# Convolution matrices built in parts, taps on other queues, and three smaller moves in the first two stages of a ConvNeXt block followed by a selective scan

## The chip, the core and the metric

The kernel runs on one core of a Trainium2 chip, in float32. The metric is device time in microseconds of one execution, and a time stands for the median of several runs. A profile is one execution recorded by the hardware profiler; its times start at the span's beginning.

## The reference, cut to what matters

Two layers, one after the other. The input x is (32, 96, 56, 56).

```python
# layer 0
h = depthwise_conv7x7(x, conv_w) + conv_b
h = layernorm over the 96 channels (ln_g, ln_b)
h = gelu(h @ w1 + b1)              # 96 -> 384
h = (h @ w2 + b2) * layer_scale    # 384 -> 96
x = h + x
# layer 1
x = silu(depthwise_conv5x5(x, conv_w) + conv_b)
dts, Bs, Cs = split(x_proj_w @ x)
delta = softplus(dt_w @ dts + dt_b)
P = exp(cumsum(max(delta * -exp(A_logs), log(1e-9))))
hs = P * cumsum(delta * Bs * x / max(P, 1e-9))
y = sum over n of hs * Cs, + x * Ds
```

The change touches layer 0, the convolution of layer 1, and the matrices of taps that both convolutions use. The scan is as it was.

## The kernel before, in words

**Units of work.** The batch is cut into two halves (g = 0, 1) of 16 images, 96 channels into 24 groups of four. A block n is one group of four channels of one half, all rows and columns. Blocks 0 to 47 are the first convolution (24 for each half), 48 to 95 the second. `convolve` multiplies the rows of a block, loaded on 31 partitions of each quarter, by banded matrices that hold the taps of a channel at every row offset; 7x7 takes 64 matmuls a block (8 column offsets x 4 quarters x 2), 5x5 takes 48. A float32 matmul appears in a profile as two passes, each with a weight load. One row of the 31 is a row of ones, which brings the bias in, and therefore the x tiles are filled with 1.0 once before the first load.

**The matrices.** `taps` loads the taps into `kt`, four times, once for each quarter of the partitions, by eight DMAs. `shifts` makes `tap` (the taps in reversed order) and `sel` (shifted identities), and returns `build`, which multiplies the two on TensorE into PSUM and copies the result into `ws[k]` (tile `w7s` or `w5s`). `bands` copies the two matrices of a block from there into the layout that `convolve` reads, on ScalarE, one or two blocks ahead.

**PSUM.** All of this work takes its PSUM from `slot`: two slots of four banks each, so all eight banks. Whoever takes a slot waits until the last reader of the one two before it is done.

**Order.** `pin` keeps every engine's instructions in program order, so the order of the code is each engine's order. Loads are issued on the queue of SP, stores on that of GpSimd, and the taps on that of ScalarE.

**First half of the time, as stages.**
- Blocks 0 to 23: a loop of `block1` (load ahead, convolve, copy to `ht` on ScalarE, store to conv1_d), `square` on ScalarE and `gather_sums` on VectorE, four additions of 128x896 into `acc`. Small setup steps of the MLP and the scan are hung behind some blocks (`later`). All matrices are built before the loop.
- The norm: blocks 24 and 25 with `norm(0)` between. It sums over the partitions by TensorE (`pm`), takes the variance and square root, and two reciprocals into `rstd_t`.
- Steps u = 0 to 56 of the MLP, `half_u` = 28 for each half. A step does, in order: `spread_norm(u+1)` (one matmul that spreads rstd into bank 3 of the slot `po`), `second(u-1)` (36 matmuls, 384 to 96), `normed(u+1)` (three multiplications on VectorE), `residual(u-1)` (bias and x, three operations on VectorE; after every second step four stores of `o` to block_d), then a block if there is one, then three times `expand` (12 matmuls and a Gelu on ScalarE). The tile `o` has one buffer; `h`, `x` have two.
- In u = 0 to 21 the block is one of 26 to 47 (first convolution, second half). In u = 22 to 27 there is no block: the second stage's taps are loaded (u = 22), `norm(1)` is done (u = 23), `shifts` (u = 24) and the matrices (u = 25 to 27). u = 28 and 29 have no block either. In u = 30 to 49 the block is one of 48 to 67 (second convolution, first half), whose Silu reads PSUM directly, with `table` loading the function's table ahead of it and the Gelu's again after it. u = 50 to 56 have no block.
- Then blocks 68 to 95 without MLP, and the scan, which takes the second half of the time.

Of the kernel before, what the change touches and what calls it, by code (L numbers as in the profile page):

```python
# [44 lines left out]
def convnext_then_scan_kernel(  # L45
# [58 lines left out]
    def taps(tmp, cw, cb, k):  # L104
        s = k + 1
        kt = tmp.tile([128, C, k], F32, name=f"kt{k}")
        pin(nc.vector.memset(kt, 0.0))
        for q in range(Q):
            lo = q * PR
            pin(nc.scalar.dma_start(  # L110
                kt[lo : lo + k], cw.rearrange("c (i u) -> i c u", i=k)
            ))
            pin(nc.scalar.dma_start(
                kt[lo + k : lo + s, :, k // 2 : k // 2 + 1],
                cb.rearrange("(o c u) -> o c u", o=1, u=1),
            ))
        return kt

    def shifts(pool, tmp, kt, k, z, zs, down):
        s = k + 1  # L120
        tap = tmp.tile([128, C, s], F32, name=f"tap{k}")
        pin(nc.vector.memset(tap[:, :, 0:1], 0.0))
        for v in range(1, s):
            pin(nc.vector.tensor_copy(tap[:, :, v : v + 1], kt[:, :, k - v : k - v + 1]))
# [18 lines left out]
        for q in range(Q):  # L143
            rows = slice(q * PR, (q + 1) * PR)
            pin(nc.vector.tensor_copy(
                sel[rows, :, :, PR - 1],
                ident[rows, q * PR + k : q * PR + s].rearrange("p (a o) -> p a o", a=1)
                .to_broadcast([PR, 2, PR]),
            ))
        wt = pool.tile([128, 2 * KB, PR * s + 1], F32, name=f"w{k}s")  # L150
# [3 lines left out]
        def build(lo, hi):  # L154
            for a in range(lo, hi):
                ps = slot(f"pw{k}_{a}")
                for i in range(Q):
                    cp, h = divmod(i, 2)
                    for b in range(Q):
                        base = tap[b * PR : b * PR + s, cp]  # L160
                        pin(nc.tensor.matmul(
                            ps[i * PR : (i + 1) * PR, b, : 2 * KB * s],
                            lhsT=sel[b * PR : b * PR + s, h, a * Q + b],
                            rhs=bass.AP(
                                base.tensor, base.offset, [base.ap[0], [2 * s, 2 * KB], [1, s]]
                            ),
                            start=True, stop=True, tile_position=(b * PR, i * PR),
                        ))
                dst = wt[:, :, a * Q * s : (a + 1) * Q * s].rearrange("p n (b v) -> p b n v", v=s)
                src = ps[:, :, : 2 * KB * s].rearrange("p b (n v) -> p b n v", v=s)  # L170
                if a % 2:
                    pin(nc.vector.tensor_copy(dst, src))
                else:
                    pin(nc.scalar.copy(dst, src))
# [216 lines left out]
    def conv(n):  # L391
# [10 lines left out]
        if k == K1:  # L402
            pin(nc.scalar.copy(ht, ps[:, :, :TOK]))  # L403
            for j in range(2):
                pin(nc.gpsimd.dma_start(  # L405
                    at(conv1_d[g], (kb * 4 + 2 * j) * CS,
                       [[2 * TOK, 64], [CS, 2], [1, 2 * TOK]]),
                    ht[j * 64 : (j + 1) * 64].rearrange("p (c h) w -> p c (h w)", c=2),
                ))
        else:  # L410
            pin(nc.scalar.activation(ht, ps[:, :, :TOK], AF.Silu))  # L411
            for j in range(2):
                for r in range(2):
                    rows = slice(j * 64 + r * PR, j * 64 + (r + 1) * PR)
                    pin(nc.gpsimd.dma_start(  # L415
                        at(conv2_d[g], (kb * 4 + 2 * j) * CS + r * 2 * TOK,
                           [[4 * TOK, PR], [CS, 2], [1, 2 * TOK]]),
                        ht[rows].rearrange("p (c h) w -> p c (h w)", c=2),
                    ))
        return ht  # L420

# [17 lines left out]
    def norm(g):  # L439
        acc = accs.pop(g)  # L440
# [11 lines left out]
        pin(nc.scalar.activation(m2, m2, AF.Sqrt, bias=eps_t, scale=1.0))  # L452
        for h in range(2):
            pin(nc.vector.reciprocal(rstd_t[:, g, h], m2[:, h]))
# [102 lines left out]
    def residual(u, po):  # L557
        n, s = divmod(u, 2)
        g, h, o = spot(n)
        for e in range(3):  # L560
            pin(nc.vector.scalar_tensor_tensor(  # L561
                ots[n][:, e].rearrange("p (t s) -> p t s", s=2)[:, :, s],
                in0=po[:, e, :TOK], scalar=b2p_t[:, e : e + 1],
                in1=xrs[n][:, e].rearrange("p (t s) -> p t s", s=2)[:, :, s],
                op0=ALU.add, op1=ALU.add,
            ))
# [17 lines left out]
    with tc.tile_pool(name="early", bufs=1) as early, tc.tile_pool(  # L584
        name="w1t", bufs=1, side="right"
    ) as tmp:
        kt = taps(tmp, c1w, c1b, K1)
        fresh += [early.tile([128, 2, COLS], F32, name=f"xe_{i}") for i in range(4)]
        for i, t in enumerate(xts + fresh):
            (nc.gpsimd if i % 2 else nc.vector).memset(t, 1.0)  # L590
        shifts(w1pool, tmp, kt, K1, Z1, (3, 0), False)(0, PR // Q)
        later = {
            2: lambda: setup_loads_mlp(tmp),
            4: setup_sums,
            6: lambda: setup_mlp_0(tmp),
# [8 lines left out]
        for n in range(KB):  # L604
            squares, sums = block1(n, half_n)
            squares()
            sums()
            if n in later:
                later[n]()
# [5 lines left out]
    for n in range(KB, KB + lead):  # L615
        squares, sums = block1(n, half_n)
        if n == KB:
            norm(0)
        squares()
        sums()  # L620
    load_x(0)
    load_h(1)
    load_x(1)

    half_u = B2 * OCT * 2
    n1, n2 = KB + lead, half_n
    start = slot("po_first")
    spread_norm(0, start[:, 3])
    normed(0, start[:, 3])
    for u in range(2 * half_u + 1):  # L630
        if u or u + 1 < 2 * half_u:
# [3 lines left out]
            if u:  # L635
                second(u - 1, po)
            if u + 1 < 2 * half_u:
                normed(u + 1, po[:, 3])
            if u:
                residual(u - 1, po)  # L640
        squares = sums = None
        if u < half_u:
# [3 lines left out]
            elif u == half_u - 6:  # L646
                wstack.close()
                w2pool = wstack.enter_context(tc.tile_pool(name="w2p", bufs=1, side="right"))
                temps = ExitStack()
                tmp = temps.enter_context(tc.tile_pool(name="w2t", bufs=1, side="right"))  # L650
                kt = taps(tmp, c2w, c2b, K2)
            elif u == half_u - 5:
                norm(1)
            elif u == half_u - 4:
                build2 = shifts(w2pool, tmp, kt, K2, Z2, (0, 3), True)
            else:
                at_ = {3: 0, 2: 3, 1: 6}.get(half_u - u)
                if at_ is not None:
                    build2(at_, min(at_ + 3, PR // Q))
                    if u == half_u - 1:  # L660
                        temps.close()
        elif u == half_u + 1:
            ahead(half_n, half_n + KB)
        elif u >= half_u + 2 and n2 < half_n + KB - TAIL:
            ahead(n2, half_n + KB)
            conv(n2)
            table(AF.Gelu)
            n2 += 1
        if u < 2 * half_u:
# [4 lines left out]
            if half_u + 2 <= u + 1 and n2 < half_n + KB - TAIL:  # L674
                table(AF.Silu)
# [303 lines left out]
```

## Time and profile before

| | us |
|---|---|
| median of 3 runs | 3306.44 (3301.59 to 3317.9) |
| the profiled execution | 3315.05 |
| its span | 3313.3 |
| block 0 begins on PE | 36.93 |
| first expansion of u = 0 | 235.66 |
| second layer's first block (48) begins | 852.74 |
| last residual ends | 1350.4 |
| scan's first matmul | 1540.7 |

| engine | busy us | share |
|---|---|---|
| PE, matmuls | 2882.4 | 87% |
| PE, weight loads | 1041.9 | 31% |
| DVE | 2129.6 | 64% |
| ACT | 1948.7 | 59% |
| POOL | 1765.8 | 53% |

How to read it. PE is TensorE, DVE VectorE, ACT ScalarE, POOL GpSimd, SP SyncE. A line of the timeline has the start, the duration, engine, line of the kernel, operation, output <- inputs, shapes and a count; in brackets stands the idle time of the engine before it and what ended it. A line of the windows has the stretch, and for each engine the busy time and count in the order PE, PEld, DVE, ACT, POOL, then the granted clock, the share of the DMA engines and GB/s. The names drop the numbers of buffers: `kt` stands for kt7 and kt5, `xc` and `xe` are tiles of x for a block, `we` the bands, `pc`, `po`, `ph`, `pm`, `pw` are slots named after their use.

### The profile page before, as it was taken

To read this page: it belongs to the slowest core of one execution; us is meant where nothing else is said; L and a number is where in the kernel's file an instruction comes from. 1 tells how busy PE (TensorE), PEld (TensorE's weight loads), DVE (VectorE), ACT (ScalarE), POOL (GpSimd) and SP (SyncE) were. 2 spreads that over 40 slices of the span, in tenths; PEclk is the share of its full clock that TensorE was granted. 3 is DMA by queue.
4 is the path that set the end of the run, shared out by engine and by line. 5 is a ranking of instruction groups with operands and counts; after the bars stand their busy time and mean duration, and the time that the engine had idled before them with its cause. 6 is when DMAs were issued, how large, how long until landed. Compare 5 with 4: busy or idle time off the path is not lost.

```text
span 3313.3 us, 65909 instructions
## 1 busy us (share of the span) xinstructions
PE 2882.4 (87%) x28172; PEld 1041.9 (31%) x28172; DVE 2129.6 (64%) x1227; ACT 1948.7 (59%) x1915; POOL 1765.8 (53%) x904
## 2 busy tenths in 40 slices
PE   7989999988999999988887888788888888887885
PEld 5544444433344443442222222222222222222221
DVE  4763333332111112100999999999999999999998
ACT  5864444433555553444766666666667666766673
POOL 2311111100111110232988988898889888987896
PEclk9999999999999999997777778777777877877776
DMA  9997666533876664697655465636564666455642
GB/s 177 267 235 210 183 185 182 168 96 109 224 199 188 190 189 126 192 280 197 179 155 148 145 184 138 165 130 182 143 173 125 183 158 157 135 174 151 161 137 87
DMA packets 363619, 563.64 MB, mean 170 GB/s; under 512 B 221728, under 2 KB 292400, under 8 KB 363328
## 3 DMA queue, kind: packets, MB, share of 16 engines
q1 hardware_dynamic: 332352, 432.29, 48.8%
q0 software_dynamic: 25424, 127.03, 12.7%
q8 instruction: 222, 3.64, 0.5%
q10 hardware_dynamic: 5552, 0.12, 0.1%
q14 instruction: 69, 0.57, 0.1%
HBM read 355.58 MB, written 203.69 MB: 169 GB/s over the span
## 4 chain that ended last, share of the span: by engine, by line
PE 45%; DVE 23%; ACT 10%; POOL 7%; DMA 5%; SPq 5%; issue 4%; ACTq 0%; POOLq 0%; DVEq 0%
PE pc L324 13%; PE po L551 11%; DVE run_t L844 9%; DVE u L852 9%; PE ph L532 8%; DVE run_t L848 5%; POOL da L859 3%; PE px L755 3%; POOL u L839 3%; PE py L871 2%; PE pz L772 2%; ACT da L830 2%; PE py L866 2%; PE pd L825 2%; SPq L383 2%
## 5 line engine op out<-in xcount | busy, mean ns | idle before, releaser
L839 POOL TENSOR_TENSOR u<-u,bc 128x1568 f32<-128x1568 f32 x192 | 674.8, 3515 | 209.2 <-DMA u<-dx_d 196.6
L844 DVE TENSOR_TENSOR_SCAN run_t<-da,run_t 128x1568 f32<-128x1568 f32 x192 | 664.5, 3461 | 68.1 <-ACT da L834 49.3
L859 POOL TENSOR_TENSOR da<-u,bc 128x1568 f32<-128x1568 f32 x192 | 674.5, 3513 | 18.8 <-DVE u L852 18.4
L524 DVE TENSOR_TENSOR h<-h,po 128x448 f32<-128x448 f32 x165 | 92.6, 617 | 588.6 <-PE po L551 554.2
L532 PE MATMUL ph<-h,w1c_t 32*128 32x448 f32 x4032 | 410.9, 551 | 29.1 <-ACT g L538 17.0
L830 ACT ACTIVATE da<-pd,lift_t,a_t 128x784 f32<-128x784 f32 x384 | 377.9, 1003 | 74.5 <-PE pd L825 64.2
L825 PE MATMUL pd<-dl,rep_t 32*128 32x392 f32 x1536 | 387.3, 641 | 32.9 <-ACT bc L807 13.7
L538 ACT ACTIVATE g<-ph,b1p_t 128x1792 f32<-128x1792 f32 x168 | 291.7, 1750 | 179.2 <-PE ph L532 160.3
L551 PE MATMUL po<-g,w_t 128*32 128x448 f32 x4032 | 390.5, 540 | 0.0
L866 PE MATMUL py<-xs,dsm_t 32*32 32x392 f32 x1536 | 251.4, 734 | 143.1 <-ACT bc L807 108.6
L324 PE MATMUL pc<-xc,we 32*64 32x432 f32 (+2 forms) x6912 | 357.6, 554 | 11.7 <-DVE h L524 7.6
L848 DVE SCALAR_TENSOR_TENSOR run_t<-run_t,u 128x1568 f32<-128x1568 f32 x192 | 345.6, 1800 | 22.2 <-POOL u L839 2.1
L571 POOL DMA_DIRECT2D block_d<-o x112 | 59.8, 557 | 547.8 <-DVE o L561 532.1
L803 PE MATMUL pk<-xd,pick_t 32*128 32x392 f32 x1024 | 270.5, 642 | 92.0 <-ACT y L877 76.5
L852 DVE TENSOR_TENSOR_SCAN u<-da,u,run_t 128x1568 f32<-128x1568 f32 x96 | 334.1, 3480 | 3.4
L852 DVE TENSOR_TENSOR_SCAN u<-da,run_t 128x1568 f32<-128x1568 f32 x96 | 328.3, 3420 | 3.3
L834 ACT ACTIVATE da<-da,lift_t 128x1568 f32<-128x1568 f32 x192 | 307.8, 1603 | 5.6
L871 PE MATMUL py<-da,sel_t 128*32 128x392 f32 x1536 | 248.4, 733 | 53.4 <-POOL da L859 53.4
L405 POOL DMA_DIRECT2D conv_d<-ht x96 | 57.1, 600 | 417.4 <-ACT ht L403 407.4
L532 PEld LDWEIGHTS ph<-h,w1c_t 32*128 32x128 f32 x4032 | 202.1, 188 | 238.0 <-issue 168.8
L415 POOL DMA_DIRECT2D conv_d<-ht x192 | 101.3, 535 | 316.5 <-ACT ht L411 292.2
L877 ACT COPY y<-py 128x392 f32<-128x392 f32 x192 | 92.0, 479 | 289.5 <-PE py L871 228.0
(118 smaller groups left out, 2993.4 us busy)
## 6 DMA issues: line engine op xcount, KB each, us to landing
u<-dx_d SPq DMA_DIRECT2D x192, 784.0 KB, 5.1
conv_d<-ht POOLq DMA_DIRECT2D x96, 448.0 KB, 6.0
conv_d<-ht POOLq DMA_DIRECT2D x192, 224.0 KB, 5.1
h<-conv_d SPq DMA_DIRECT2D x336, 112.0 KB, 2.8
x<-in_x_dram SPq DMA_DIRECT2D x112, 336.0 KB, 8.8
block_d<-o POOLq DMA_DIRECT2D x112, 336.0 KB, 7.1
xs<-conv_d SPq DMA_DIRECT2D x384, 98.0 KB, 4.0
dx_d<-dx SPq DMA_DIRECT2D x256, 147.0 KB, 3.3
```

What stands on the lines that cost most here:

```text
L324: pin(nc.tensor.matmul(pv[:, :, lo:hi], lhsT=wt[rows, j, k - d], rhs=xv[rows, j, :, lo + e : hi + e, s], start=(t == 0), stop=(t == k), ti ...
L532: pin(nc.tensor.matmul(ph[:, q, :TOK], lhsT=w1c_t[quarter(q), e, f * 128 : (f + 1) * 128], rhs=ht[quarter(q), e, s], start=(e == 0), stop= ...
L551: pin(nc.tensor.matmul(po[quarter(q), e, :TOK], lhsT=w2_t[:, f, e * PR : (e + 1) * PR], rhs=gts[u, f][:, q], start=(f == 0), stop=(f == 2) ...
L825: pin(nc.tensor.matmul(ps[:, j, :BK], lhsT=rep_t[quad(q)].rearrange("p c n -> p (c n)"), rhs=dls[b, h][quad(q), g], start=True, stop=True, ...
L830: pin(nc.scalar.activation(pair(da, a), ps[:, :, :BK], AF.Relu, bias=lift_t[:, 0:1], scale=a_t[:, g : g + 1],))
L839: pin(nc.gpsimd.tensor_mul(us[i], us[i], bcs[b, h, 0]))
L844: pin(nc.vector.tensor_tensor_scan(run_t[:, 1 : T + 1], da, zero, run_t[:, T : T + 1] if h else 1.0 / EPS, ALU.mult, ALU.add,))
L848: pin(nc.vector.scalar_tensor_tensor(run_t[:, :T], in0=run_t[:, 1 : T + 1], scalar=1.0, in1=ut, op0=ALU.min, op1=ALU.mult,))
L852: pin(nc.vector.tensor_tensor_scan(ut, da, run_t[:, :T], last["h"] if h else 0.0, ALU.mult, ALU.add))
L859: pin(nc.gpsimd.tensor_mul(das[i], us.pop(i), bcs[b, h, 1]))
L866: pin(nc.tensor.matmul(py[quad(j)], lhsT=dsm_t[quad(j), g], rhs=tokens(b, h, quad(j), g), start=True, stop=False, tile_position=(j * PR, j ...
L871: pin(nc.tensor.matmul(py[quad(j)], lhsT=sel_t, rhs=hc[:, j * BK : (j + 1) * BK], start=False, stop=True, tile_position=(0, j * PR),))
```

## The change

Five things change.
1. The matrices are built in parts. `build(n0, cnt, a0, per)` now makes `cnt` groups from `n0`, and `4 * per` offsets from `a0`, in one slot. A matmul has cnt x s columns (64 or 128 in the first stage, 144 in the second, instead of 384 and 288), and there are 512 instead of 128 in the first stage and 256 instead of 128 in the second. A slot is emptied in two halves, one by ScalarE and one by VectorE. In the first stage only groups 0 to 7 are built before block 0; five more parts follow blocks 0, 1, 4, 6 and 10. In the second stage six parts stand in u = 23 to 28.
2. The taps go by ScalarE's and SP's queues in turn in the first stage, by SP's alone in the second. All tiles of ones are filled by GpSimd, and `tap` is made after the shifted identities.
3. In steps with no block (u = 22 to 29 and 50 to 56, where `mixed` is false) ScalarE adds the bias, reading PSUM and writing `o`, and GpSimd then adds x.
4. In u = 30 to 49 ScalarE copies the block raw out of PSUM, and Silu runs in place behind the step's three Gelus, with its table loads and the stores.
5. At the first norm the order is: variance, Sqrt straight into `rstd_t`, one reciprocal, then block 25, both `spread_norm` and `normed`, then the sums and the second reciprocal. At the second one `moments(1)` moves to u = 22, `spans` and `inverse` behind that step's Gelus.

```diff
-    def taps(tmp, cw, cb, k):
+    def taps(tmp, cw, cb, k, queues):
...
-            pin(nc.scalar.dma_start(
+            queue = queues[q % len(queues)]
+            pin(queue.dma_start(
                 kt[lo : lo + k], cw.rearrange("c (i u) -> i c u", i=k)
             ))
...
-        def build(lo, hi):
-            for a in range(lo, hi):
-                ps = slot(f"pw{k}_{a}")
+        def build(n0, cnt, a0, per):
+            ps = slot(f"pw{k}_{n0}_{a0}")
+            for r in range(per):
                 for i in range(Q):
                     cp, h = divmod(i, 2)
                     for b in range(Q):
-                        base = tap[b * PR : b * PR + s, cp]
+                        base = tap[b * PR : b * PR + s, cp + 2 * n0]
+                        to = ps[i * PR : (i + 1) * PR, b, r * s : r * s + 1]
                         pin(nc.tensor.matmul(
-                            ps[i * PR : (i + 1) * PR, b, : 2 * KB * s],
-                            lhsT=sel[b * PR : b * PR + s, h, a * Q + b],
+                            bass.AP(to.tensor, to.offset, [to.ap[0], [per * s, cnt], [1, s]]),
+                            lhsT=sel[b * PR : b * PR + s, h, a0 + b * per + r],
...
+            for e in range(2):
+                half = slice(2 * e, 2 * e + 2)
+                lo = (a0 + 2 * e * per) * s
+                dst = wt[:, n0 : n0 + cnt, lo : lo + 2 * per * s]
+                src = ps[:, half, : cnt * per * s].rearrange("p b (n v) -> p n b v", n=cnt)
+                copy = nc.vector.tensor_copy if e else nc.scalar.copy
+                pin(copy(dst.rearrange("p n (b v) -> p n b v", b=2), src))
...
+    def silu(n, ht):
+        pin(nc.scalar.activation(ht, ht, AF.Silu))
+        put2(n, ht)
...
-    def norm(g):
+    def moments(g):
...
-        pin(nc.scalar.activation(m2, m2, AF.Sqrt, bias=eps_t, scale=1.0))
-        for h in range(2):
-            pin(nc.vector.reciprocal(rstd_t[:, g, h], m2[:, h]))
+
+    def spans(g):
+        m2 = accs.pop(g)[:, 0]
+        pin(nc.scalar.activation(rstd_t[:, g], m2, AF.Sqrt, bias=eps_t, scale=1.0))
+
+    def inverse(g, h):
+        pin(nc.vector.reciprocal(rstd_t[:, g, h], rstd_t[:, g, h]))
...
-    def residual(u, po):
+    def residual(u, po, plain):
...
+            if plain:
+                pin(nc.scalar.activation(
+                    ot[:, e], po[:, e, :TOK], AF.Identity, bias=b2p_t[:, e : e + 1], scale=1.0
+                ))
+            else:
+                pin(nc.vector.scalar_tensor_tensor(
+                    ot[:, e], in0=po[:, e, :TOK], scalar=b2p_t[:, e : e + 1], in1=xr[:, e],
+                    op0=ALU.add, op1=ALU.add,
+                ))
+        if plain:
+            pin(nc.gpsimd.tensor_add(ot, ot, xr))
...
-        kt = taps(tmp, c1w, c1b, K1)
+        kt = taps(tmp, c1w, c1b, K1, (nc.scalar, nc.sync))
...
-        for i, t in enumerate(xts + fresh):
-            (nc.gpsimd if i % 2 else nc.vector).memset(t, 1.0)
-        shifts(w1pool, tmp, kt, K1, Z1, (3, 0), False)(0, PR // Q)
+        for i in range(4):
+            for t in (xts[i], fresh[i]):
+                pin(nc.gpsimd.memset(t, 1.0))
+        build1 = shifts(w1pool, tmp, kt, K1, Z1, (3, 0), False)
+        build1(0, 8, 0, 8)
+        rest = {
+            0: (8, 16, 0, 4), 1: (8, 16, 16, 4), 4: (24, 16, 0, 4), 6: (24, 16, 16, 4),
+            10: (40, 8, 0, 8),
+        }
...
+            if n in rest:
+                build1(*rest[n])
...
-    for n in range(KB, KB + lead):
-        squares, sums = block1(n, half_n)
-        if n == KB:
-            norm(0)
-        squares()
-        sums()
+    squares, sums = block1(KB, half_n)
+    moments(0)
+    spans(0)
+    inverse(0, 0)
+    squares()
     load_x(0)
     load_h(1)
     load_x(1)
-
-    half_u = B2 * OCT * 2
-    n1, n2 = KB + lead, half_n
+    squares_1, sums_1 = block1(KB + 1, half_n)
     start = slot("po_first")
     spread_norm(0, start[:, 3])
     normed(0, start[:, 3])
+    po = slot("po_0")
+    spread_norm(1, po[:, 3])
+    normed(1, po[:, 3])
+    sums()
+    inverse(0, 1)
+    squares_1()
+    sums_1()
+
+    builds = [(n0, 24, a0, 3) for n0 in (0, 24) for a0 in (0, 12)]
+    builds += [(n0, 24, 24, 2) for n0 in (0, 24)]
     for u in range(2 * half_u + 1):
+        mixed = u < half_u and n1 < half_n or u >= half_u + 2 and n2 < half_n + KB - TAIL
...
-                residual(u - 1, po)
+            residual(u - 1, po, not mixed)
...
+                k = u - half_u + 6
+                if k == 0:
...
+                    kt = taps(tmp, c2w, c2b, K2, (nc.sync,))
+                    build2 = shifts(w2pool, tmp, kt, K2, Z2, (0, 3), True)
+                    moments(1)
+                elif builds:
+                    build2(*builds.pop(0))
+        elif u < half_u + 2:
+            if builds:
+                build2(*builds.pop(0))
...
-            conv(n2)
-            table(AF.Gelu)
+            held = (n2, conv(n2, raw=True))
             n2 += 1
...
-            if half_u + 2 <= u + 1 and n2 < half_n + KB - TAIL:
-                table(AF.Silu)
+        if held is not None:
+            table(AF.Silu)
+            silu(*held)
+            table(AF.Gelu)
+        if u == half_u - 6:
+            spans(1)
+            for h in range(2):
+                inverse(1, h)
```

## The prediction

> **What bounds the kernel now.** I read the page, the stages by windows, then chain and timelines of PE, DVE and ACT around each place that the diff touches. The page's slices show PE busy nearly throughout the first half and DVE after it; the diff touches only the first half, up to about 1350 us, and what it saves there shifts the rest. The first half is five stages.
>
> Stage A, blocks 0 to 23 of the first convolution (to 197.6). PE starts late and, at the end, waits for x:
>
> ```profile
> 19.21 9.00 PE L161 MATMUL pw<-tap,shift 8*32 8x384 f32 x160 [19.21 <-DVE shift L145]
> 36.93 28.28 PE L324 MATMUL pc<-xc,we 32*64 32x448 f32 x503 [3.19 <-ACT we L349]
> 191.11 6.02 PE L324 MATMUL pc<-xe,we 32*64 32x448 f32 x113 [2.50 <-DMA xe<-in_x_dram]
> 20.00:40.00 20.00, 15.81 (x282) 5.48 (x284) 7.13 (x5) 10.38 (x9) 0.00 (x0) 1.00 1.02 144
> 120.00:140.00 20.00, 20.00 (x424) 11.81 (x416) 12.91 (x13) 17.80 (x14) 13.84 (x26) 1.00 0.95 272
> ```
>
> Lines four and five are windows: the last column is GB/s, the one before it DMA share. Loads alone move 144 GB/s, loads with stores up to 272; both fill the engines. So a late start of PE is only partly lost: loads run ahead and PE eats the lead up.
>
> Stage A to B, the norm:
>
> ```profile
> 213.92 5.76 DVE L454 RECIPROCAL rstd_t<-acc 128x448 f32<-128x448 f32 x2 [2.45 <-ACT acc L452]
> 225.99 1.68 DVE L524 TENSOR_TENSOR h<-h,po_first 128x448 f32<-128x448 f32 x3
> 227.72 8.01 PE L324 MATMUL pc<-xc,we 32*64 32x448 f32 x128 [7.62 <-DVE h L524]
> ```
>
> Between reciprocals and L524 stand six channel sums (219.72 to 225.99); PE's next block waits for L524, whose PSUM slot it takes.
>
> Stage B, u = 0 to 21, repeats each 21.05 us with PE full; nothing in it changes. Stage C, u = 22 to 29, has no block:
>
> ```profile
> 706.63 3.40 ACT L538 ACTIVATE g<-ph,b1p_t 128x1792 f32<-128x1792 f32 x2 [18.90 <-DMA kt<-in_c2b_dram]
> 708.43 4.27 PE L532 MATMUL ph<-h,w1c_t 32*128 32x448 f32 x24 [9.72 <-ACT g L538]
> 824.30 4.79 PE L532 MATMUL ph<-h,w1c_t 32*128 32x448 f32 x48 [1.21 <-DVE o L561]
> ```
>
> The second stage's taps are issued on ACT ahead of a step's Gelus (9.72 us), and in every step the residual on DVE, queued behind the multiplications by the norm, holds PE 1.21 us. Stage D, u = 30 to 49, repeats each 20.1 us with one wait; stage E, u = 50 to 56, has the 1.21 again and ends in a chain:
>
> ```profile
> 862.78 2.54 PE L532 MATMUL ph<-h,w1c_t 32*128 32x448 f32 x24 [0.33 <-ACT g L538]
> 1348.55 1.87 DVE L561 SCALAR_TENSOR_TENSOR o<-po,b2p_t,x 128x448 f32<-128x448 f32 x3 [12.01 <-PE po L551]
> 1350.71 2.13 POOL L571 DMA_DIRECT2D block_d<-o x4 [25.52 <-DVE o L561]
> ```
>
> After that last store the remaining blocks are fed by loads of block_d, so its time passes to the end.
>
> **Stage A, head: +5 us.** Taps on two queues: the eight DMAs were issued from 1.60 to 9.3 on ACT, the last landing at 15.5 (DVE's copies start there). Four a queue at about 0.6 each are issued by 4.0; with the last one's 5.9 landing they are there near 10. SP then starts x later, but in the built order each of the first eight x loads waits for the landing of one tap DMA, as most did before, and the eighth leaves near 10 in both. Edge and shift copies (3 us) now precede the tap copies, hidden; the memsets, all on POOL (8 x 1.59 from 2.8), reach xc_1 at 7.6, before SP wants it. So: copies 10 to 11.2, first part of the matrices (below) 2.5, two evictions side by side of 1024 elements (1.54 and 1.76 for 1536, so 1.0 and 1.2), bands 1.1: PE starts its blocks near 16.5 instead of 36.9, 20.4 earlier. The other four parts come back into the stream.
>
> The price of a part: a float32 matmul is two passes; the first part has 128 matmuls of 64 columns (256 passes), the rest 384 (768 passes). The nearest rows:
>
> ```profile
> 756.93 0.79 PE L161 MATMUL pw<-tap,shift 6*32 6x288 f32 x32
> 756.90:757.10 0.20, 0.17 (x16) 0.17 (x32) 1.00 0.00 0
> ```
>
> Sixteen passes and 32 loads start within 0.17 us, 11 ns each; 32 passes of 288 columns with drain are 0.79, 25 each. With 11: 768 passes are 8.4 us. PE alone would then end block 23 at 16.5 + 8.4 + the 151 that blocks 0 to 22 took + 6.3 = 182, 15 us sooner. Loads will not let it: stores now start 20 us sooner. If the sum of traffic is the limit, 20.4 us at about 258 instead of 144 GB/s (means of the windows) is 2.3 MB, 9 us. If loads merely lose what the stores take (SP's queue moved 144 GB/s alone, 9.88 MB from 100 to 190 us, 110 GB/s, beside stores), 20.4 x 34 GB/s are 0.69 MB, 6 us at that pace: -6. I take +5, between the two and nearer to the first, since the share from 60 to 200 us was 0.93 and not full; bounds -6 to +15.
>
> The Trainium skill ("TensorE: Matmul & The Clock Gate", section "Wait — 56ns, not 53.3ns?") speaks against cutting the matmuls small: start to start never falls below about 25 ns. By it 1024 passes cost 26 us, PE alone would end block 23 only 1 us sooner, and the whole sum below would be some 23 us instead of 30. The row above, 11 ns over different tiles, does not show that floor, and I go by the row.
>
> **Norm: +5.5.** In the new order one reciprocal (2.9) ends at 216.9 and the multiplications come before the sums. What is late next is h: SP issues its twelve loads until 218.1 and they land 3.0 later, 221.1; the last multiplication ends near 222 and block 26 starts there, not at 227.7. The sums, second reciprocal and square follow behind block 26 (8 us); ACT's square waits for one sum, ends near 228, just ahead of the copy it precedes. SP's loads of x and h(1) move ahead of x for block 28, which is wanted only at 266. Bounds 3.5 (h late) to 7 (the 8.01 of block 26 falls to the 6.4 of others).
>
> **Stage C: +11.** At u = 22 PE goes on at 692.43. The taps go to SP after h(12); DVE's memset no longer follows a residual, so they start near 694.8 and, with the same 10 us of issue and landing near 709 less 1.8, are there at about 707.5. New wait: DVE's tap copies stand before the variance, and the third expansion takes the slot of the sums pm, which the variance frees: 707.5 + 0.9 + 1.1 = 709.5. ACT's Gelus are free but PE stops there instead, 7 us. u = 22 ends near 719.7 (27.3 against 27.85, now with pm's 3.27 inside). u = 23: Sqrt behind the Gelus, reciprocals (5.76) until 722, multiplications till 723.8, then PE: 18.9. u = 24 to 28: 14.86 unstalled (16.07 less 1.21) plus a wait for the multiplications that covers the part, 1.85: 16.7 each. u = 29: four bands (3.2) now stand behind the bias on ACT and delay a Gelu: 16.7. Sum 147, against 160.3 (692.43 to 852.74): 13. Two expansions of before took 9.4 and 9.7 at a clock of 0.84 instead of 7.05; whether that recurs I cannot see, so I take 11, bounds 6 to 15. A taps landing later costs its lateness in full.
>
> The bias on ScalarE: no row; by the PSUM copies (479 for 392 columns, 1650 for 1792) three of 448 are 1.58, beside the multiplications' 1.69 and both under the first expansion's 2.45: the 1.21 is gone. GpSimd's sum of 1344 elements: 3.0 by L839 (3.515 for 1568), 3.4 by the strided dx row (2.96 for 1176); I take 3.2. It delays the store, and o has one buffer: the next tile's bias waits for it on ACT ahead of the Gelus. 1.6 + 3.3 + 1.6 + a median landing of 7.1 = 13.6, inside a step of 14.9.
>
> **Stage D: +5.6.** The wait of 0.28 on average (5.6 over 20) goes: a copy (1.65) replaces Silu (1.66), and table load, Silu, table load (4.6) move behind the third Gelu beside 7.7 of PE. **Stage E: +2.6.** Five waits of 1.21 are 6.05; the last residual costs 1.58 + 3.2 instead of 1.87, -2.9 straight into the last chain; -0.5 for late landings of o (longest 10.7). Bounds -1 to 4.
>
> **Sum:** 5 + 5.5 + 11 + 5.6 + 2.6 = 29.7. The profiled execution took 3315.05 (span 3313.3): 3285.4. It lies 8.6 above the median of the runs, 3306.44, and the forecast by that is 3276.7.
>
> **Rivals.**
> 1. The loads eat the head start: stage A at -6, everything else as above: 18.7 gained, 3287.7. For it: the share of 1.02 before any store. Against: 0.93 later, and PE waiting for x only at 188. Chance 0.18.
> 2. The taps land late on SP: the wait that replaces ACT's. 10 us later than 707.5, stage C gains 1, and the total is 3286.7. Chance 0.08.
> 3. PE alone sets stage A: +15, total 39.7, 3266.7. Chance 0.12.
> 4. Slower: a small pass costs what a large one does, 48 ns as in a block (128 passes in 6.2 us). Place: the matmuls of `build` (L163 once changed) between blocks and in u = 23 to 28. Without parts PE alone ends block 23 at 182.2 - 2.5 - 8.4 = 171.3; 1024 passes at 0.048 are 49, so 220.5: stage A at -23. In stage C a part of 96 passes costs 4.6 and one of 64 3.1 instead of 1.85: -14. Total 29.7 - 5 - 23 - 14 = -12, 3318.7. The total turns negative from about 41 ns a pass, and is over 0.5% slower from 51. Against: 25 ns with drain. Chance 0.07.
> The forecast itself: 0.55.
>
> **Numbers.** About 0.5% (16.5 us) is what a measurement here tells from no change: 3289.9. The forecast's bounds, combined as independent, are about 12 either way; cases 1 and 2 lie inside that, 3 at its edge, 4 outside, and the runs themselves spread by 16, so I go a little past it on the slow side, where three cases lie: 3262 to 3298. Faster by over 0.5%: 0.95 of the forecast, half of 1 and 2, all of 3: 0.77; slower 0.05 (the part of 4 over 51 ns, and the tails); the rest is within 0.5%, 0.18.
>
> **What would show it.** Right: first block near 16.5; block 26 within a microsecond of the last h; no 1.21 in steps without a block, no 0.3 in stage D; the third expansion of u = 22 waiting for DVE. Wrong: gaps `<-DMA xc` early in stage A, L163 over 5 us for a part, a bias waiting for block_d, block 23 ending after 198.

## The result, and the profile after

The changed kernel takes 3329.07 us (median; 3316.62 to 3336.99) against 3311.35 us of before in the same sessions (3301.59 to 3318.53): ratio 1.0049, 95% interval 1.0032 to 1.0065. It is slower by 18 us; 30 us faster was forecast. The two profiled executions lie only 1.5 us apart (spans 3314.8 and 3313.3), because the second half, which the diff doesn't touch, is 12.4 us shorter in the profile of after. Over the twelve profiles of this study, from the first matmul on an `xd` buffer to the end, it took 1932 to 1946 us with no order in it. So the parts are weighed on the first half, by marks in the trace: the start of ACT's copy of block 23 out of PSUM (A ends), block 26's first matmul (the norm ends), the starts of the third Gelu of u = 21, 29 and 49 (C and D lie between them), and the first matmul on `xd` (E ends).

| us | before | after | gain | forecast |
|---|---|---|---|---|
| A, to the copy of block 23 | 197.59 | 216.69 | -19.1 | +5 |
| norm | 30.13 | 21.98 | +8.2 | +5.5 |
| rest of the first step, and stage B | 458.25 | 458.65 | -0.4 | 0 |
| C, u = 22 to 29 | 159.31 | 162.74 | -3.4 | +11 |
| D, u = 30 to 49 | 402.01 | 390.53 | +11.5 | +5.6 |
| E, to the first matmul on `xd` | 120.09 | 130.80 | -10.7 | +2.6 |
| sum | 1367.38 | 1381.39 | -14.0 | +29.7 |

How far one profile can be trusted shows where several share the same code of a stage. Three profiles with stage A of before end it at 193.1 to 197.6, four with that of after at 215.9 to 221.9; stage E as in the kernel after took 126.9 to 130.8 in five, and the norm of before 28.4 and 30.1 in two. Differences of a few microseconds in A, the norm or E say little by themselves.

Three stages did worse than forecast, two better. First the head of the kernel, from timelines of DVE, POOL and PE:

```profile
1.78 12.34 DVE L133 COPY edge<-ident 32x7 f32<-32x7 f32 x4
11.98 1.59 POOL L615 MEMSET xe<- 128x1792 f32 x1
17.90 3.25 PE L163 MATMUL pw<-tap,shift 8*32 8x64 f32 x223 [17.90 <-DVE tap L150]
24.89 0.54 PE L163 MATMUL pw<-tap,shift 8*32 8x64 f32 x33 [3.74 <-issue]
29.11 9.41 PE L327 MATMUL pc<-xc,we 32*64 32x448 f32 x128 [3.67 <-issue]
```

Four tiny copies that took 0.69 before take 12.34: the first of them is held for 11.80, until the last of GpSimd's eight memsets ends (13.6), the other three take 0.16 each. The first part stops for 3.74 us after 223 of its 256 passes, and block 0 starts at 29.11, 7.8 us sooner than before instead of 20. The part's two evictions run one behind the other (ACT's and DVE's timelines):

```profile
25.60 1.02 ACT L177 COPY w7s<-pw 128x1024 f32<-128x1024 f32 x1 [19.90 <-PE pw L163]
26.64 1.22 DVE L177 COPY w7s<-pw 128x1024 f32<-128x1024 f32 x1 [8.72 <-ACT w7s L177]
```

Then two of the parts between blocks (PE's timeline):

```profile
72.08 1.37 PE L163 MATMUL pw<-tap,shift 8*32 8x128 f32 x83
74.79 1.36 PE L163 MATMUL pw<-tap,shift 8*32 8x128 f32 x45 [1.34 <-issue]
126.02 2.03 PE L163 MATMUL pw<-tap,shift 8*32 8x64 f32 x185
131.83 1.32 PE L163 MATMUL pw<-tap,shift 8*32 8x64 f32 x71 [3.78 <-issue]
```

And windows of 2 us over the first of them (columns: stretch; its length; PE, PEld, DVE, ACT and POOL busy; granted clock; DMA share; GB/s):

```profile
72.00:74.00 2.00, 1.45 (x87) 1.02 (x84) 0.12 (x2) 1.76 (x2) 1.86 (x4) 1.00 0.85 177
74.00:76.00 2.00, 1.21 (x45) 0.78 (x44) 1.97 (x2) 1.59 (x1) 0.01 (x1) 0.69 0.60 136
76.00:78.00 2.00, 2.00 (x29) 0.86 (x32) 1.97 (x3) 1.81 (x2) 1.06 (x2) 0.50 1.06 177
78.00:80.00 2.00, 2.00 (x32) 0.71 (x24) 1.37 (x2) 1.27 (x2) 1.36 (x3) 0.50 0.98 303
80.00:82.00 2.00, 2.00 (x40) 0.77 (x32) 0.00 (x0) 0.00 (x0) 0.00 (x0) 0.60 1.00 344
82.00:84.00 2.00, 2.00 (x48) 0.77 (x40) 0.00 (x0) 0.00 (x0) 0.00 (x0) 1.00 1.01 350
```

Each of these two parts is cut in two by a stop, and the clock is granted at half about it: by the trace's clock record from 74.8 to 81.6 and from 129.4 to 136.2, 6.8 us each (and for 3.4 from 95.2, behind the part at 91.85; not behind those at 38.45 and 50.28). Meanwhile 29 to 32 passes of the convolution fall into 2 us instead of 48. From block 0 to block 23 PE no longer waits for x; it is the bound, and the lost time lies in its own stops and at half clock.

The norm goes as planned, with h next in line (DVE, then PE):

```profile
236.93 1.68 DVE L541 TENSOR_TENSOR h<-h,po_first 128x448 f32<-128x448 f32 x3 [2.73 <-DMA h<-conv_d]
238.67 7.80 PE L327 MATMUL pc<-xc,we 32*64 32x448 f32 x120 [0.40 <-DVE h L541]
```

A step of stage C, all engines (timeline):

```profile
750.61 1.68 DVE L541 TENSOR_TENSOR h<-h,po 128x448 f32<-128x448 f32 x3 [16.46 <-PE po L568]
752.38 1.72 ACT L581 ACTIVATE o<-po,b2p_t 128x448 f32<-128x448 f32 x3 [7.60 <-DVE h L541]
754.15 8.69 PE L549 MATMUL ph<-h,w1c_t 32*128 32x448 f32 x72 [2.12 <-ACT o L581]
754.18 3.63 POOL L590 TENSOR_TENSOR o<-o,x 128x1344 f32<-128x1344 f32 x1 [18.19 <-ACT o L581]
```

The chain at the end of stage E (timeline), and one line of ACT's waits from 1255 to 1350 (total, times, longest):

```profile
1359.66 1.73 ACT L581 ACTIVATE o<-po,b2p_t 128x448 f32<-128x448 f32 x3 [5.09 <-PE po L568]
1361.46 3.71 POOL L590 TENSOR_TENSOR o<-o,x 128x1344 f32<-128x1344 f32 x1 [10.03 <-ACT o L581]
1365.47 2.15 POOL L595 DMA_DIRECT2D block_d<-o  x4 [0.30 <-POOL o L590]
```
```profile
ACT o L581 <- DMA block_d<-o: 24.2, 3, 10.2
```

The bias starts only when the three multiplications have ended, so the two do not lie side by side: in the trace its first activation waits for VectorE's last read of the same PSUM slot (of another bank; why it has to wait is not shown). The expansions behind it take 8.69 instead of 7.05, again partly at half clock (0.50 from 754 to 756). In stage E ACT stands idle three times, 24.2 us in all, until the stores of o have landed and the bias may start. The expansions of u = 23 and of u = 51 behind such waits (PE's timeline; 48 passes take 4.79 at full clock):

```profile
732.34 7.05 PE L549 MATMUL ph<-h,w1c_t 32*128 32x448 f32 x48 [4.37 <-ACT o L581]
1278.94 6.49 PE L549 MATMUL ph<-h,w1c_t 32*128 32x448 f32 x48 [2.20 <-ACT o L581]
```

In stage D the three expansions now run without a stop:

```profile
872.41 7.05 PE L549 MATMUL ph<-h,w1c_t 32*128 32x448 f32 x72
```

### The profile page after: what moved, and what is told of

Its sections match the earlier page's. It is cut to its first block, busy times and chain, and to the rows that moved or that the text cites. A ratio compares the mean times of both kernels' runs of the same rounds, so it can differ in the third digit from the quotient of the medians.

```text
span 3314.8 us, 68041 instructions
## 1 busy us (share of the span) xinstructions
PE 2876.8 (87%) x29196; PEld 1042.6 (31%) x29196; DVE 2111.5 (64%) x1182; ACT 2008.2 (61%) x1984; POOL 1827.1 (55%) x923
## 4 chain that ended last, share of the span: by engine, by line
DVE 28%; PE 10%; POOL 8%; ACT 5%; DMA 4%; issue 4%; SPq 3%; POOLq 0%; DVEq 0%; ACTq 0%
DVE u L898 11%; DVE run_t L890 11%; DVE run_t L894 6%; POOL da L905 3%; POOL u L885 3%; SPq L386 2%; PE px L801 2%; PE py L917 2%; ACT da L876 2%; DMA xd<-block_d 1%; PE pc L327 1%; PE py L912 1%; POOL dx L833 1%; PE pd L871 1%; PE pz L818 1%
## 5 line engine op out<-in xcount | busy, mean ns | idle before, releaser
L327 PEld LDWEIGHTS pc<-xc,we 32*64 32x64 f32 x6912 | 174.0, 131 | 184.9 <-issue 171.6
```

The costliest lines, as they stand in the source:

```text
L327: pin(nc.tensor.matmul(pv[:, :, lo:hi], lhsT=wt[rows, j, k - d], rhs=xv[rows, j, :, lo + e : hi + e, s], start=(t == 0), stop=(t == k), ti ...
```

## The experiments

Each ratio is to the kernel before, in the same session; for the kernel after it is 1.0049.

**Silu behind the Gelus, alone.** Before, with this:

```diff
-            conv(n2)
-            table(AF.Gelu)
+            held = (n2, conv(n2, raw=True))
...
+        if held is not None:
+            table(AF.Silu)
+            silu(*held)
+            table(AF.Gelu)
```

> The kernel before with one part of the change: the raw copy in the step, Silu with its table loads and stores behind the third Gelu (stage D). Theory (the parts add up, and this one is a plain gain): the 20 steps u = 30 to 49 go from 20.10 to 19.53 us each as in the kernel after, block 68 starts 11 us sooner than the 1348.4 of before, and the time falls by about 11, to 0.9966 of before. Rival (stage D gains only because something earlier was late, or what follows is bound by loads): the steps stay near 20.1, or block 68 starts sooner and the time does not fall.

3293.59 us, 0.9961 (0.9945 to 0.9978). The steps of stage D take 19.53, those of before 20.06 and 20.14 in turn; the first half of the profile is 13.4 shorter, stage D 11.4 of it. The part is a plain gain, and stage D is not bound by loads.

**The order at the norm, alone.** Before, with `norm` cut into `moments`, `spans` and `inverse`, and the block between load_h(0) and the loop as in the kernel after.

> The kernel before with one part of the change: the order at the first norm (one reciprocal, multiplications ahead of the channel sums, second reciprocal and square behind). Theory: block 26 starts 23.0 us after block 23's end instead of 30.15, a gain of 7, all of it in the time (0.998). Rival (the x loads, moved behind more of SP's loads, are late in the next steps): the 7 us come back as waits for x or h within the first steps of stage B, and the time stays.

3301.16 us, 0.9972 (0.9955 to 0.9989). Block 26 starts 24.74 behind the copy of block 23 (30.13 before): here h lands later, and PE waits for its multiplication 4.0 instead of 0.4:

```profile
217.89 9.51 PE L324 MATMUL pc<-xc,we 32*64 32x448 f32 x128 [4.03 <-DVE h L528]
```

A gain, and nothing of it comes back as a wait for x: through the steps up to u = 21 PE waits for no load. The loads of h are its limit.

**Residual on VectorE in every step.** After, with

```diff
-            residual(u - 1, po, not mixed)
+            residual(u - 1, po, False)
```

> The kernel after with the residual on VectorE in every step, as before (no bias on ScalarE, no sum on GpSimd). Theory (the bias starts only when VectorE's three multiplications have ended, it stands ahead of the Gelus, and in every other step it waits for the stores of o behind a GpSimd sum of 3.6 us): stage C, 163.7 us in the kernel after, falls to about 152, and stage E, 101.4, to 93.6 as before; in all some 19 us, 0.994 of after. Rival (stages C and E are long through the granted clock of 0.91 and the parts of the matrices, not through the bias): stage C stays above 160 and stage E above 98.

3319.78 us, 1.0036 (1.0021 to 1.0052): by the two ratios 4 us below after, where 19 were expected, and the intervals overlap. Stage E is 120.8, 10.0 less than after, and u = 29 takes 16.09 instead of 18.64. But stage C as a whole is 168.3, longer by 5.6: u = 24 to 27 stay at 20.0, where the rival was right, and u = 22 takes 29.85 instead of 21.65:

```profile
726.37 4.86 PE L549 MATMUL ph<-h,w1c_t 32*128 32x448 f32 x24 [7.64 <-DVE acc L463]
```

In this profile everything up to here is some 4 us later. Without the GpSimd sum ahead of them the stores of o start with the taps (711.9 and 712.1), and these are there only at 724.4; in the kernel after the taps start at 706.2, the stores at 711.4, and the taps are there by 714.2. So the bias costs 12.5 at u = 29 and in stage E together, and saves 8.2 at u = 22.

**First matrices whole.** After, with

```diff
-        build1(0, 8, 0, 8)
+        for a in range(0, PR, Q):
+            build1(0, 2 * KB, a, 1)
...
-            if n in rest:
-                build1(*rest[n])
```

> The kernel after with the first stage's matrices built whole ahead of block 0: eight pieces of 16 matmuls of 384 columns (256 passes in all, as before) instead of six parts of 128 matmuls of 64 or 128 columns (1536 passes), five of them between blocks. Theory (the small matmuls outrun PE's supply of instructions, each part stops PE for 1 to 3.8 us, and the clock is granted at half for some us behind it): block 0 starts later, near 35 instead of 29.1, yet block 23 ends near 197 instead of 215.7, no wait of L163 is put down to issue between blocks, the clock is 1.00 throughout, and the time falls by about 18, 0.9945 of after. Rival (loads that start later and stores beside them set stage A, whatever PE does): block 23 ends at 207 or later, with PE waiting for x.

3297.31 us, 0.9972 (0.9961 to 0.9984); by the two ratios some 25 us below after. (The expectation's 1536 passes are too many: the first and the last part have 128 matmuls, the four others 64, 1024 passes in all.) PE's timeline, then a window:

```profile
28.82 3.23 PE L163 MATMUL pw<-tap,shift 8*32 8x384 f32 x64 [0.41 <-DVE w7s L177]
35.15 5.43 PE L327 MATMUL pc<-xc,we 32*64 32x448 f32 x45 [3.09 <-issue]
```
```profile
120.00:140.00 20.00, 20.00 (x420) 12.59 (x409) 14.13 (x14) 17.86 (x14) 13.44 (x26) 1.00 1.01 260
```

Block 0 starts at 35.15, 6 us later than in the kernel after, and the copy of block 23 starts at 192.09, 24.6 sooner. The clock is 1.00 from 40 to 200. (In every profile here the clock's record begins some 4 to 7 us behind block 0's start. The windows ahead of it print 1.00, but in the kernel after, for one, 10 to 13 passes start in a microsecond there, and some 20 behind it.) The parts are the loss of stage A, and with them gone the sign of the whole change turns.

**Memsets shared out.** After, with

```diff
-        for i in range(4):
-            for t in (xts[i], fresh[i]):
-                pin(nc.gpsimd.memset(t, 1.0))
+        for i, t in enumerate(xts + fresh):
+            (nc.gpsimd if i % 2 else nc.vector).memset(t, 1.0)
```

> The kernel after with the eight memsets of x buffers shared out as before (four on VectorE, four on GpSimd) instead of all on GpSimd. Theory (VectorE's copies stand still while GpSimd's memsets run: the four 32x7 copies took 12.34 us, to 14.1, where GpSimd's last memset ends at 13.6): the four copies fall to about 0.7, the first tap copy starts near 12 instead of 16.7, block 0 near 24.5 instead of 29.1, and block 23 ends some 4.5 us sooner, 212. Rival (the copies waited for ident or were slowed by loads, or the loads bind): the copies stay above 5 us, or block 0 starts sooner and block 23 does not end sooner.

3316.51 us, 1.0025 (1.0011 to 1.004). DVE's timeline:

```profile
7.51 1.55 DVE L614 MEMSET xe<- 128x1792 f32 x1 [0.32 <-issue]
9.28 0.69 DVE L133 COPY edge<-ident 32x7 f32<-32x7 f32 x4
12.52 1.18 DVE L150 COPY tap<-kt 128x96 f32<-128x96 f32 x7
```

The copies take 0.69 again, the taps are there when they end, block 0 starts at 24.97, and the copy of block 23 at 211.73, 5.0 sooner, and 4.1 sooner than in any of the four profiles with after's stage A. VectorE's memsets (1.55 each) ran beside GpSimd's at their own pace; in the kernel after its copies did not. The same at u = 22: two copies took 4.38 beside a GpSimd sum in the kernel after (first two lines), and 1.30 without it in the run with the residual on VectorE (third line):

```profile
707.49 3.63 POOL L590 TENSOR_TENSOR o<-o,x 128x1344 f32<-128x1344 f32 x1 [15.06 <-ACT o L581]
707.88 4.38 DVE L137 COPY shift<-edge 128x1024 f32<-128x1024 f32 x2
713.86 1.30 DVE L137 COPY shift<-edge 128x1024 f32<-128x1024 f32 x2
```

**Short runs.** After, with the last three parts cut into twelve:

```diff
-            0: (8, 16, 0, 4), 1: (8, 16, 16, 4), 4: (24, 16, 0, 4), 6: (24, 16, 16, 4),
-            10: (40, 8, 0, 8),
+        rest = {0: (8, 16, 0, 4), 1: (8, 16, 16, 4)}
+        rest.update({2 + i: (24, 16, 4 * i, 1) for i in range(8)})
+        rest.update({10 + i: (40, 8, 8 * i, 2) for i in range(4)})
```

> The kernel after with the same matmuls in the parts of the first stage, but the last 384 of them cut into twelve short runs: eight of 16 (behind blocks 2 to 9) and four of 32 (behind blocks 10 to 13), instead of three of 128; the first part and the two behind blocks 0 and 1 stay as they are. Theory (a long run of small matmuls outruns PE's supply of instructions; the stop then halves the granted clock): from block 2 on no matmul of L163 waits by issue, the clock is 1.00 there, and block 23 ends 15 to 20 us sooner than the 216.7 of after. Rival (the price is per matmul or per column, wherever they stand, or each extra eviction holds a block): block 23 ends at 210 or later.

3333.71 us, 1.0083 (1.0067 to 1.0098): the copy of block 23 starts at 234.18, 17.5 later than in the kernel after. The theory fell as it stood. (The three parts have 64, 64 and 128 matmuls, 256 in all, and not the expectation's 384.) PE's timeline:

```profile
80.08 0.50 PE L163 MATMUL pw<-tap,shift 8*32 8x128 f32 x32
81.89 8.40 PE L327 MATMUL pc<-xe,we 32*64 32x448 f32 x128 [1.31 <-ACT ht L406]
```

Of the twelve runs only one was stopped inside, for 0.89, but each costs 2 to 4 us all the same. The program has two slots in PSUM: a part takes one, so the next block needs the slot of the block just finished, and PE waits 1.31 for ACT's copy of it. Behind that wait the block takes 8.4 instead of 6.8, at a clock of 0.83 over the step; behind the last four runs, with waits of 0.77 to 0.96, it takes 6.5 to 6.8, at 1.00. In a long part the part itself covers that copy. So the price of a part is its run, a wait (for issue or for the slot), and often a stretch at half clock.

**Second stage's parts behind the first expansion.** After, with

```diff
-                elif builds:
-                    build2(*builds.pop(0))
...
                 expand(u, f)
+                if f == 0 and u > half_u - 6 and builds:
+                    build2(*builds.pop(0))
```

> The kernel after with the second stage's parts moved behind the first expansion of their step instead of ahead of it. Theory (ahead of it, PE waits 2.1 us for the readers of po and the clock is then granted at 0.5 for some 4 us, which costs 1.6 more; behind it, that wait is 1.2 as in a step without a part, and the clock stays): steps u = 24 to 27 fall from 20.0 to about 17.7 with the clock at 1.00, stage C is some 12 us shorter, 0.9965 of after. Rival (the clock falls in stage C for another reason, such as little work on the chip as a whole, or the part's eviction holds the third expansion): the steps stay at 19 or more.

3311.94 us, 1.0008 (0.9996 to 1.0021). u = 24, 26 and 27 take 17.7, u = 25 and 28 take 19.4; stage C is 157.2 instead of 162.7. In u = 24 the clock is 1.00 throughout, with a wait of 1.15; in u = 25, with 1.22, it still fell (PE's timeline, then a window):

```profile
761.06 1.56 PE L163 MATMUL pw<-tap,shift 6*32 6x144 f32 x96 [1.15 <-ACT o L581]
778.80 1.56 PE L163 MATMUL pw<-tap,shift 6*32 6x144 f32 x96 [1.22 <-ACT o L581]
```
```profile
782.00:784.00 2.00, 2.00 (x14) 0.90 (x12) 0.39 (x1) 0.00 (x0) 0.48 (x1) 0.50 0.00 0
```

In u = 27 a wait of 1.22 left the clock at 1.00, in u = 28 one of 1.15 did not: no fixed length of wait decides whether it falls. In stage C this is half of what was expected, 5.5 of 12. The two ratios say 14 us in all; where the rest lies, these profiles don't show (stage A of this one is 5 longer than after's, stage E 4 shorter, with the same code).

**Bias in the even half alone.** After, with

```diff
-            residual(u - 1, po, not mixed)
+            residual(u - 1, po, not mixed and u % 2 == 1)
```

> The kernel after with the bias on ScalarE in the even half of the tile (s = 0) alone; the half that the stores follow goes to VectorE as before, so stores do not wait for a GpSimd sum. Theory (stage E loses through o's single buffer: the bias of the next tile waits for stores that start behind the sum): steps u = 51 and 53 fall from 18.85 and 21.27 to about 16.1, no bias waits for block_d for more than a microsecond, and the chain at the end of stage E is shorter by some 3 us; u = 29, whose bias stays, keeps its 18.6. Rival (the bias itself, late behind the multiplications and ahead of the Gelus, is the price): u = 51, 53 and 55 stay above 18.

3322.56 us, 1.0054 (1.0033 to 1.0075). u = 51 and 53 take 16.15 and 16.09 (18.85 and 21.27 after), no bias waits for block_d, and stage E is 120.1, as before. u = 29 keeps 18.66, and u = 22, whose residual is again on VectorE, takes 29.81; that is why the total does not fall. PE's waits in stage E, by whoever reads `po` last:

```profile
1270.16 4.79 PE L549 MATMUL ph<-h,w1c_t 32*128 32x448 f32 x48 [1.21 <-DVE o L585]
1286.24 4.79 PE L549 MATMUL ph<-h,w1c_t 32*128 32x448 f32 x48 [1.22 <-ACT o L581]
```

The bias itself gains nothing and costs nothing in stage E; the loss there was the single buffer of o behind the GpSimd sum.

**Two combinations.** After with whole matrices, shared memsets, VectorE's residual, the second stage's parts behind the first expansion, and the taps' memset and DMAs ahead of the residual of u = 22; then the same with the taps back in their place and the bias on ScalarE at u = 22 alone.

> A combination: the kernel after with the first stage's matrices whole ahead of block 0, memsets shared out as before, the residual on VectorE in every step, the second stage's parts behind the first expansion, and its taps started ahead of the residual of u = 22. The norm's order and Silu behind the Gelus stay. If the parts add up: block 23 ends near 188, stage C is 12 to 15 us and stage E 8 us shorter than in the kernel after; together some 50 us below after, 0.990 of before. If they do not add (loads bind once PE is early), block 23 ends above 193 and the total stays above 0.993 of before.

3283.89 us, 0.9927 (0.9908 to 0.9945). Block 0 starts at 30.95, 4.2 sooner than with whole matrices alone, and the copy of block 23 at 193.86, not sooner (192.09): PE waits 2.8 for xe, and the clock is at half for 3.4 about that. In this profile the loads bind. u = 22 took 29.05: SP sent three of the eight taps' DMAs, then twelve loads of h, then the other five beside the stores of o, and the tap copies could start only at 696.6, 15.6 behind the end of the step's last products (681.0).

> The combination again, with the taps of the second stage where the kernel after has them and the bias on ScalarE in step u = 22 alone (there it lets the taps start before the stores of o); every other residual is on VectorE. Theory (the bias is a gain at u = 22, where it brings the taps in some 8 us sooner, and a loss of 2.5 us at u = 29 and of 8 in stage E): u = 22 takes 21.7 us as in the kernel after instead of 29.05, stage E stays at 93.6, and the time falls by about 7 below the first combination, to 0.990 of before. Rival (the taps are late for another reason, such as loads that start sooner here): u = 22 stays above 26.

3275.48 us, 0.991 (0.9891 to 0.993): the fastest version, 31 us below before and, by the ratios, some 46 below after. u = 22 takes 21.78, stage C 148.1, and block 23's copy starts at 190.18: with the same code up to there as the first combination, 3.7 sooner, and with 0.4 of waiting for xe. What the start of block 0, sooner by 4.2, is worth lies within what profiles of the same code differ by.

## Why the prediction was wrong, step by step

**The price of a part: wrong, and the cause of the sign.** The step "With 11: 768 passes are 8.4 us" took its price from a run of 16 passes and used it for runs of 128 and 256 (five parts; the prediction speaks of four, but counts their passes rightly). From the first matmul of a part to the next block the five parts took 3.71, 2.31, 4.00, 3.16 and 7.06, together 20.2: 7.7 of it stops by issue, the rest 16 ns a pass. Blocks 0 to 23 took 187.6 in all, against 156.9 with whole matrices, so 10 more went to the half clock, the waits around the parts and their slots. In the four profiles with this stage A the clock was at half for 13.7 to 27.3 us of it; with the matrices whole ahead of block 0 for none in five profiles and for 3.4 in one. Rival 4 had the place right and the mechanism wrong: it is not the single pass that is dear.

What stops PE inside a part was not tried by itself. What speaks for the supply of instructions: at each of the five stops in the first stage (the first part's among them) the trace's instruction queue has a packet of 16 KB that lands (at 23.26, 39.90, 73.34, 92.74 and 130.26) 1.4 to 1.6 us before the matmuls go on (24.89, 41.50, 74.79, 94.14, 131.83); at the one part that was not stopped (50.28) such a packet lands at 50.39, as it begins; and the whole build with its 256 passes of 384 columns shows no stop by issue. The Trainium skill ("Runtime: NRT & Kernel Launch", section "Instruction fetch mechanics") says that an engine's stream is refilled in blocks of 16 KB, 256 instructions, and that this is mostly hidden; if these landings are what PE stopped for, then here, with two weight loads and two passes to a matmul at 16 ns a pass, it was not hidden. The floor of 25 ns from start to start that the prediction weighed (the Trainium skill, "TensorE: Matmul & The Clock Gate", section "Wait — 56ns, not 53.3ns?") isn't what these rows show either: between the stops the passes took 11 to 19 ns each, and the loss lay in the stops and behind them.

**Head: 12.6 us late** (29.1 for 16.5). The taps did land early, but the edge copies, called hidden, ended at 14.1: 6.7. The first part took 7.5 for 2.5: 5.0. The two evictions, taken as side by side, ran one after the other: most of the rest (the prediction's own terms add up to 16.0, not 16.5). The memset step looked only at SP's need for xc_1, not at VectorE beside GpSimd. The Trainium skill ("SBUF — State Buffer", section "Who interferes with whom") has that rule: a VectorE instruction in a mode that uses both its ports and a GpSimd instruction shut each other out. The 12.34 against 0.69 agree with it; that these copies use both ports no run here shows, and the first of them waited out all of the memsets that followed each other, not one.

**Do loads eat the head start?** Rival 1 was not met, since PE never got that early. The combinations answer it in part: with block 0 at 30.95 or 35.15 block 23 was copied at 190.2 to 193.9, with waits of PE for x of 2.8 in one profile, 0.4 in another and none in the third. So its mechanism sets in about there. That the 15 us of PE alone could not have come is likely, but no run started block 0 near 16.5.

**Norm: right, and larger** (8.2, bounds 3.5 to 7; 6.4 against the other profile with the norm of before). h was next in line, as said: 5.4 alone, with 4.0 of waiting for it, and 8.2 in the kernel after, with 0.4.

**Stage C: wrong** (-3.4 for 11). u = 22 was better than forecast, 22.6 for 27.3 (by the prediction's mark on PE; 21.65 by the Gelus): the taps landed in time because the stores of o came behind them. u = 23 took 24.1 for 18.9, the largest miss of a single step: the late bias held the expansions by 1.8, the half clock about PE's wait of 4.37 cost 2.3 more (7.05 for 4.79), and the Gelu's table, loaded again behind the Sqrt (1.28), held the third expansion by 0.97. u = 24 to 27, each with a part, took 20.0 instead of 16.7, u = 28 18.3: the base of 14.86 supposed that the bias lay beside the multiplications, and a wait of 2.1 brought the half clock (1.6) with it. With the residual on VectorE these steps took the same, so moving the bias bought nothing there. u = 29 took 18.6 for 16.7: the bands behind the late bias delayed a Gelu by more than forecast. The clock of 0.84, seen in two expansions of before and left out as "whether that recurs I cannot see", was the term to chase.

**Stage D: the mechanism right, the size half** (11.5 for 5.6). The wait was priced at the 0.28 that its row calls idle. But in the rows matmuls overlap: an expansion of 24 passes is given 2.54 and three in a row take 7.05, so each begins 0.28 ahead of the end of the one before it. A wait gives up that overlap too: 0.57 a step, 11.4 over 20.

**Stage E: wrong** (-10.7 for +2.6). "13.6, inside a step of 14.9" counted a median landing of 7.1 for the last of the four stores and a sum of 3.2: they took 9.7 and 11.2, and 3.6, at the two tiles where it mattered. From the start of a bias to the next one on its tile buffer that is 17 to 18.7 us, in steps that take 16.1. So u = 51 and 53 took 18.85 and 21.27 instead of 16.1: PE waited 2.20 and 3.79 for the bias instead of 1.2, and the half clock behind these waits cost 1.7 and 2.6 more. The five waits of 1.21 did not go either, since the bias starts behind the multiplications as the residual did. From the last Gelu to the first matmul on `xd` it is 28.6 for 25.7, the 2.9 that was forecast for the chain at the end.

## What to carry to other kernels

Price a run of small matmuls from a run as long as the one you mean to build, and add what its slot and its stop do to the work behind it: here a wait of PE from about 1 us on could bring 3.4 or 6.8 us at half clock. Before work goes to an idle engine, look at what it will stand behind there (a read of the same slot, a port, a single buffer), for idle is not the same as free. When a change has several parts, run them one by one: two of these were gains of 7 and 14 us that the sum hid.

## What the runs showed of the hardware that was not expected

- Runs of 64 or 128 small matmuls (128 or 256 passes with their weight loads) stopped PE for 1.0 to 3.8 us in five parts of six; pieces of 32 wide passes (384 columns) did not stop inside.
- The granted clock fell to 0.50 behind waits of PE as short as 0.96 us (the stop that ends at 94.14), but not every time: the stop of 1.60 that ends at 41.50 left it at 1.00, one wait of 1.31 between blocks at 0.97, and waits of 1.15 to 1.22 mostly at 1.00. In all twelve traces the clock's record knows 1.00 and 0.50 alone and changes only on a grid of 3.41 us, so a fall lasts 3.41 us or a multiple of it. That may be why equal waits end differently, according to how they lie on that grid; it was not tried.
- A copy on VectorE stood still for as long as GpSimd's memsets ran back to back (11.80 of the 12.34 that four copies took, for 0.69); VectorE's memsets did not (1.55 each beside GpSimd's).
